# Routing a mixture in quarters of the tokens: more of the next layer beside the expert slots of a two-layer kernel on one core

## The chip, the cores and the metric

The kernel runs on one core of a Trainium2 chip. The metric is the device time of one execution in microseconds (us), taken as the median of several runs; the profile is of one execution, and its span runs from the first to the last instruction of the core. PE is the matrix engine (PEld its weight loads), DVE the vector engine, ACT the scalar engine, POOL the general engine, SP the engine that only issues transfers here.

## The reference

All data are float32. `x` is 2 x 1024 tokens of 256 features, `ctx` 2 x 77 context rows. Two layers of the same shape follow each other:

```python
x = x + L0_xattn(ctx, layernorm(x), ...)      # 16 heads of 64, keys and values from tokens and context
x = x + L0_ffn(layernorm(x), ...)             # 8 experts 256 -> 1024 -> 256 with relu, the best 2 per token, then a norm
x = x + L1_xattn(layernorm(x), ctx, ctx, ...) # 16 heads of 16, queries from tokens, keys and values from the context
x = x + L1_ffn(layernorm(x), ...)             # 8 experts, the best 2: four gated MLPs (256 -> 128 -> 256, silu),
                                              # two copies of x, one relu(x), one zero; plus a causal depthwise conv of width 4
```

In the reference `L0_ffn` computes all experts for all tokens and weighs them; only the two chosen ones have a weight.

## The kernel before

The 2048 tokens are 16 tiles `t` of 128 tokens (8 per batch), four tiles are a block (`NBLK = 4`). `xr` holds the running sum of all tokens in SBUF. Four stages follow each other.

**Layer 0's attention** is the first 1158 us; the change does not touch its code, only what waits for its buffers. Beside it, tokens of blocks 0 and 1 are already routed: each token is scattered twice, once per chosen expert, into the DRAM table `tab_x`, where each expert has its own rows.

**The slots** compute the layer-0 experts. A slot is 128 rows of one expert: `NSLOT = 39` of them hold every case of how tokens spread over experts. Which expert and which rows a slot has is computed on the chip: `first_table` (blocks 0 and 1 alone) for the first `NA = 9` slots, `table` for the rest, ordered so that after `NB = 23` slots all rows of batch 0 are done. `ask_rows(s)` loads a slot's rows into `xs`, and `ask(s)` its bias `bs` and its two weight matrices `w1` and `w2` (1 MB each), all on SP's queue, three slots ahead; `entry` reads the address from the table. `turn_rows` transposes the rows (`px`, then `xT` on DVE), `up` is the first matmul in two halves (`ph`; relu of half 0 on DVE, of half 1 on ACT, into `hT`), `down` the second (`po`), run one slot later; ACT copies the result `y` and stores it to the DRAM table `tab_y`. Weights rotate through four buffers (`fw`, `fw_x`), and through two from slot 30 on. PSUM has 8 banks: three `ps_t` for short transposes and products, two `ps_h`, one `ps_o`, and two more (`ps_x`) that the slots use as a third `ph` and a second `po` bank.

**Per tile, after its slots**: `gather(t)` fetches the two expert results of each token by indirect DMA on POOL's queue, `weigh` adds them, `measure`, `residual`, `shift` and `normal` are the norms around it, `turned` and `queries` make the transposed queries `qT` of layer 1. `todo` lists, by slot, what runs behind a slot; tile `t` of batch 0 is gathered behind slot `NB + t`. For batch 1 the residual is `residual_aside`, on ACT and POOL.

**Layer 1's attention** goes in steps: step `k` is one tile and half of the heads (`score`, `soften`, and one step later `turn_step`; `attend` for a pair `p` of tiles; then `divide`, `turn_back`, `project` per tile). From slot `S1 = 31` on there are two steps per slot, one between the halves of `up` and one behind `down`; when the slots end, at step `K1 = 16`, the steps run alone: the tail. `pre`, `fill` and `rest` hold, by step, what else runs: `pre` before the scores, `fill` and `rest` after the softmax.

**Layer 1's experts** (`Mix`, one per block): `measure`, `values`, `turns`, `choose` (the routing), then for each of four experts `up` (`pg`, silu on ACT, `hid` on DVE) and `down` (`po`, added to `xr` by DVE with the token's weight); `copies` adds the copy and relu experts for one tile, `convolve` and `convolved` the convolution. `at_step` sets the steps: block 0's at 16 to 23, block 1's at every second step from 24 to 38, blocks 2 and 3 at 42 to 57.

PE, DVE, ACT, POOL and, in the slots and after, SP issue in the order written here (`manual_schedule`). An instruction that waits holds those behind it on its engine.

Of the kernel before, what the change touches and what calls it, by code (L numbers as in the profile page):

```python
# [38 lines left out]
NB = 2 * S // TB + E0 - 1  # L39
NK = CAP // TB  # L40
# [9 lines left out]
def tile_two_layers(ctx: ExitStack, tc: tile.TileContext, a: dict, out: bass.AP):  # L50
# [938 lines left out]
    def apart_from(ins, mine, other):  # L989

        tc.declare_no_dep(ins.ins, group=other, reason="rows of other tokens")
        tc.add_to_no_dep_group(mine, ins.ins)

    def gather(t):

        got[t] = []
        for k in range(2):
            y = en.tile([P, D], F32, tag="yt", name="yt", bufs=6)
            ins = nc.gpsimd.indirect_dma_start(  # L999
                out=y,  # L1000
                out_offset=None,
                in_=tab_y[:, :],
                in_offset=bass.IndirectOffsetOnAxis(ap=pos[:, t, k : k + 1], axis=0),
            )
            if t < NT // B:
                apart_from(ins, "gathers", "late_stores")
            got[t].append(y)
# [22 lines left out]

    def residual_aside(t):

        nb, rstd = stat.pop((0, t))
        nc.scalar.activation(acc(t), acc(t), AF.Identity, bias=nb[:, :1], scale=rstd[:, :1])
        nc.gpsimd.tensor_tensor(acc(t), acc(t), gamma, ALU.mult)
        nc.gpsimd.tensor_tensor(xr[:, t, :], xr[:, t, :], acc(t), ALU.add)
# [50 lines left out]
    S1 = 31  # L1087
    K1 = 2 * (NSLOT - S1)
    K2 = K1 + 10
# [5 lines left out]
    slots, extra, first, spare = ExitStack(), ExitStack(), ExitStack(), ExitStack()  # L1095
    fw = slots.enter_context(tc.tile_pool(name="fw", bufs=2, reuse_waits="tile"))
    xp = slots.enter_context(tc.tile_pool(name="b_x", bufs=3, reuse_waits="tile"))
    hp = slots.enter_context(tc.tile_pool(name="b_h", bufs=2, reuse_waits="tile"))
    yp = slots.enter_context(tc.tile_pool(name="b_y", bufs=2, reuse_waits="tile"))

    fw_x = extra.enter_context(tc.tile_pool(name="fw_x", bufs=2, reuse_waits="tile"))
    xe = first.enter_context(tc.tile_pool(name="b_xe", bufs=1, side="right", reuse_waits="tile"))
    ps_x = spare.enter_context(tc.tile_pool(name="b_ps_x", bufs=1, space=PSUM, reuse_waits="tile"))
    at_p = ps_s = mp = None
    later = {}

    def table():

        some, took = plan1["some"], plan1["took"]
        every = blocks(xp, "c", counts(NBLK), 0, NK, ALU.is_gt)  # L1110

        n = xp.tile([1, 2, E0], F32, tag="n", name="n", bufs=1)
        nc.vector.tensor_tensor(n[:, 0, :], some, took, ALU.subtract)
        nc.vector.tensor_tensor(n[:, 1, :], every, some, ALU.subtract)
        cum = xp.tile([1, 2, E0], F32, tag="cum", name="cum", bufs=1)
        nc.vector.tensor_copy(cum, n)
        for e in range(1, E0):
            nc.vector.tensor_tensor(cum[:, :, e : e + 1], cum[:, :, e - 1 : e], n[:, :, e : e + 1], ALU.add)
        nc.vector.tensor_tensor(cum[:, 1, :], cum[:, 1, :], cum[:, 0, E0 - 1 :].to_broadcast([1, E0]), ALU.add)
        yield  # L1120

        d = xp.tile([1, 2, E0], F32, tag="d", name="d", bufs=1)
        nc.vector.tensor_tensor(d, n, cum, ALU.subtract)
        nc.vector.tensor_tensor(d[:, 0, :], d[:, 0, :], took, ALU.add)
        nc.vector.tensor_tensor(d[:, 1, :], d[:, 1, :], some, ALU.add)
        d = d.rearrange("o k e -> o (k e)")
        step = xp.tile([1, 2 * E0], F32, tag="step", name="step", bufs=1)
        nc.vector.tensor_copy(step, d)
        nc.vector.tensor_tensor(step[:, : 2 * E0 - 1], d[:, 1:], d[:, : 2 * E0 - 1], ALU.subtract)
        cum = cum.rearrange("o k e -> o (k e)")  # L1130
        le = xp.tile([1, NL, 2 * E0], F32, tag="le", name="le", bufs=1)
        nc.vector.tensor_tensor(
            le,
            cum.unsqueeze(1).to_broadcast([1, NL, 2 * E0]),
            slot[:1].unsqueeze(2).to_broadcast([1, NL, 2 * E0]),
# [5 lines left out]
        nc.vector.tensor_tensor(le, le, step.unsqueeze(1).to_broadcast([1, NL, 2 * E0]), ALU.mult)  # L1141
# [6 lines left out]
        nc.vector.tensor_tensor(used, slot[:1], cum[:, 2 * E0 - 1 :].to_broadcast([1, NL]), ALU.is_lt)  # L1148
        nc.vector.tensor_tensor(off, off, used, ALU.mult)
        nc.vector.tensor_scalar_mul(off, off, float(TB))  # L1150
        nc.vector.tensor_scalar(used, ex[:, 0, :], float(E0), -float(E0), ALU.is_ge, ALU.mult)
        nc.vector.tensor_tensor(ex[:, 0, :], ex[:, 0, :], used, ALU.add)
# [13 lines left out]
    def ask_rows(s):  # L1166

        r0 = entry(nc.sync, s, 1)
        if s < NA:
            xs = xe.tile([P, D], F32, tag=f"xs{s}", name="xs", bufs=1)  # L1170
        else:
            xs = xp.tile([P, D], F32, tag="xs", name="xs")
        nc.sync.dma_start(out=xs, in_=tab_x[bass.ds(r0, TB), :])
        rows_of[s] = xs

    def ask(s):

        e = entry(nc.sync, s, 0)
        bs = xp.tile([P, NF], F32, tag="bs", name="bs", bufs=4)
        nc.sync.dma_start(out=bs, in_=a["L0_ffn_b1"][:, bass.ds(e * NF, NF)])  # L1180
        pool = fw_x if s % 4 > 1 and s < S1 - 1 else fw
        w1 = pool.tile([P, 2, F0], F32, tag="w1", name="w1")
        nc.sync.dma_start(
            out=w1,
            in_=a["L0_ffn_W1"][bass.ds(e, 1)].rearrange("o k f -> (o k) f").rearrange("(c p) f -> p c f", p=P),
        )
        w2 = pool.tile([P, NF, D], F32, tag="w2", name="w2")
        nc.sync.dma_start(
            out=w2,
            in_=a["L0_ffn_W2"][bass.ds(e, 1)].rearrange("o f d -> (o f) d").rearrange("(c p) d -> p c d", p=P),  # L1190
        )
        parts[s] = bs, w1, w2

    def turn_rows(s):
# [4 lines left out]
        xT = xp.tile([P, 2, TB], F32, tag="xT", name="xT")  # L1199
# [3 lines left out]
    def hidden(s):  # L1203
        return hp.tile([P, NF, TB], F32, tag="hT", name="hT")

    def up(s, xT, hT, half):
        bs, w1, w2 = parts[s]
        f4 = half * 4
        pool = ps_x if (2 * s + half) % 3 == 2 and s < S1 else ps_h
        ps = pool.tile([P, 512], F32, tag="h", name="ph")  # L1210
# [18 lines left out]
    def down(s, hT):  # L1229
        w2 = parts.pop(s)[2]  # L1230
        ps = (ps_x if s % 2 and s < S1 else ps_o).tile([P, 512], F32, tag="o", name="po")
# [6 lines left out]
        if s >= NB:  # L1238
            apart_from(ins, "late_stores", "gathers")
# [44 lines left out]
    def soften(t, c, sc):  # L1284
        pr = pr_of[t, c] = at_p.tile([P, 8, C], F32, tag="pr", name="pr", bufs=3)
# [28 lines left out]
    def attend(p, c):  # L1314
# [12 lines left out]
        raw = raw_of[p, c] = at_p.tile([P, 2, 2 * P], F32, tag="raw", name="raw", bufs=4)  # L1327
# [18 lines left out]
    def turn_back(t):  # L1346
# [4 lines left out]
        aT = aT_of[t] = at_p.tile([P, 2 * P], F32, tag="aT", name="aT", bufs=2)  # L1351
# [14 lines left out]
    class Mix:  # L1366
# [69 lines left out]
        def copies(self, i):  # L1436

            t, h, cw = self.tiles[i], self.h[:, i, :], self.cw
            y = mp.tile([P, D], F32, tag="y", name="y")
            nc.gpsimd.tensor_scalar_mul(y, h, cw[:, i, EM : EM + 1])  # L1440
            nc.gpsimd.tensor_tensor(xr[:, t, :], xr[:, t, :], y, ALU.add)
            nc.gpsimd.tensor_scalar(h, h, 0.0, cw[:, i, EM + 3 : EM + 4], ALU.max, ALU.mult)
            nc.gpsimd.tensor_tensor(xr[:, t, :], xr[:, t, :], h, ALU.add)

        def convolve(self, c):

            if c == 0:
                self.cv = mp.tile([P, 2, 512], F32, tag="cv", name="cv", bufs=2)
# [18 lines left out]
        def up(self, e):  # L1467
            ps = []
            for w in (wg1, wu1):
                ups[0] += 1  # L1470
                pool = ps_x if ps_x is not None and ups[0] % 3 == 0 else ps_h
                ps.append(pool.tile([P, 512], F32, tag="h", name="pg"))
                for c in range(2):
                    nc.tensor.matmul(  # L1474
                        ps[-1],
# [5 lines left out]
            sl = mp.tile([P, 512], F32, tag="sl", name="sl", bufs=2)  # L1481
            nc.scalar.activation(sl, ps[0], AF.Silu)
            hid = self.hid[e] = mp.tile([P, 512], F32, tag="hid", name="hid", bufs=2)
            nc.vector.tensor_tensor(hid, sl, ps[1], ALU.mult)

        def down(self, e):
            hid = self.hid.pop(e)
            po = [
                ps_o.tile([P, 512], F32, tag="o", name="po"),
                ps_t.tile([P, 512], F32, tag="t", name="po")  # L1490
                if ps_x is None
                else ps_x.tile([P, 512], F32, tag="o", name="po"),
            ]
# [20 lines left out]
    ups = [0]  # L1514
# [4 lines left out]

    todo = {  # L1520
        0: [r3.values, r3.turns],
        1: [r3.choose],
        2: [r3.place] + [lambda r=r, i=i: r.scatter(i) for r in (r2, r3) for i in range(4)],
        5: [r2.weigh],
        6: [r3.weigh],
        7: [r2.bias_turn],
        8: [r2.bias_add, r3.bias_turn],
        9: [r3.bias_add],
# [7 lines left out]
    for k in (3, 4, 4):  # L1536
        behind(k, next, steps)
    behind(10, constants, 0)
    behind(11, lambda: spread.setdefault("s", side_spread()))
    behind(14, constants, 1)  # L1540
    behind(20, constants, 2)
    behind(S1 + 1, constants, 3)
    for blk in range(NBLK):
        behind(13 + 2 * blk, shifts, blk)
    for t in range(NT // B):
        n = NB + t
        behind(n, gather, t)
        behind(n + 2, weigh, t)
        behind(n + 2, measure, 0, t)
        behind(n + 3, residual, t)  # L1550
        behind(n + 3, measure, 1, t)
        behind(n + 4, shift, 1, t)
        behind(n + 4, normal, t)
        behind(n + 5, turned, t)
        behind(n + 6, queries, t)


    pre, fill, rest, step_of = {}, {}, {}, {}
# [3 lines left out]

    for p in range(NT // 2):
# [38 lines left out]
    for blk in range(NBLK):  # L1602
        for e in range(EM):
            halves.append((blk, e))
# [148 lines left out]
```

## Time and profile before

| | |
|---|---|
| device time, median of 3 runs (all of them) | 1761.82 us (1760.5, 1761.82, 1764.8) |
| the profiled execution: its time, its span | 1765.13 us, 1763.4 us |
| mean granted clock of PE in it | 0.98 |
| instructions in it | 25084 |
| busy: PE, DVE, ACT, POOL | 1649.9, 1073.9, 715.3, 899.1 us |
| moved by DMA | 151.94 MB |

How to read it: the page gives for each engine the time in which it executed something; a busy PE is not a PE at its peak, since matmuls overlap and the clock can be lower. In its 40 slices (44 us each) a digit is the busy share in tenths, and `PEclk` is the clock granted to PE in tenths. A row of a timeline is: start, duration, engine, line, operation, output<-input, shape, count, and in brackets the idle time before it and what ended that. The line numbers are those of the listing above.

### The profile page before, as it was taken

To read this page: it belongs to the slowest core of one execution; us is meant where nothing else is said; L and a number is where in the kernel's file an instruction comes from. 1 tells how busy PE (TensorE), PEld (TensorE's weight loads), DVE (VectorE), ACT (ScalarE), POOL (GpSimd) and SP (SyncE) were. 2 spreads that over 40 slices of the span, in tenths; PEclk is the share of its full clock that TensorE was granted. 3 is DMA by queue.
4 is the path that set the end of the run, shared out by engine and by line. 5 is a ranking of instruction groups with operands and counts; after the bars stand their busy time and mean duration, and the time that the engine had idled before them with its cause. 6 is when DMAs were issued, how large, how long until landed. Compare 5 with 4: busy or idle time off the path is not lost.

```text
span 1763.4 us, 25084 instructions
## 1 busy us (share of the span) xinstructions
PE 1649.9 (94%) x9346; PEld 1052.9 (60%) x9346; DVE 1073.9 (61%) x2133; ACT 715.3 (41%) x1393; POOL 899.1 (51%) x586
## 2 busy tenths in 40 slices
PE   6999999999999999999999999889999989967887
PEld 3544555555555555565555555568898877744554
DVE  5766766666666667677767766644221554476466
ACT  1544444445444444434444445401121244426541
POOL 1277557757756765776757757212300410176124
PEclk9999999999999999999999999999999999989898
DMA  3011211211211210000000000069889956210000
GB/s 115 24 56 61 80 60 68 72 66 66 84 66 66 72 49 7 13 6 7 18 7 1 17 9 1 1 201 364 290 302 322 321 170 198 91 30 25 1 13 24
DMA packets 124862, 151.94 MB, mean 86 GB/s; under 512 B 13211, under 2 KB 112709, under 8 KB 124741
## 3 DMA queue, kind: packets, MB, share of 16 engines
q1 hardware_dynamic: 79984, 102.18, 17.2%
q10 hardware_dynamic: 41685, 39.77, 6.5%
q0 software_dynamic: 3072, 8.39, 1.4%
q8 instruction: 74, 1.21, 0.3%
q14 instruction: 47, 0.39, 0.1%
HBM read 105.10 MB, written 45.22 MB: 85 GB/s over the span
## 4 chain that ended last, share of the span: by engine, by line
PE 71%; DVE 12%; ACT 7%; POOL 6%; DMA 2%; issue 2%; SPq 0%; ACTq 0%; DVEq 0%
PE sc L745 13%; PE ptr L797 12%; PE po L822 8%; PE po L1233 7%; PE ph L1214 7%; PE pqk L675 7%; DVE nm L755 5%; POOL pa L779 4%; ACT pa L756 4%; PE pv L651 3%; PE py L690 3%; PE pg L1474 3%; PE ptr L1308 1%; PE sb L720 1%; ACT pT L117 1%
## 5 line engine op out<-in xcount | busy, mean ns | idle before, releaser
L779 POOL TENSOR_SCALAR pa<-pa,f 128x1024 f32<-128x1024 f32 x244 | 695.8, 2869 | 363.9 <-ACT pT L117 259.7
L756 ACT ACTIVATE pa<-sc,nm 128x1024 f32<-128x1024 f32 x256 | 283.1, 1110 | 424.6 <-DVE nm L755 424.6
L755 DVE TENSOR_REDUCE nm<-sc 128x1 f32<-128x1024 f32 x256 | 301.4, 1219 | 137.0 <-PE sc L745 137.0
L797 PE MATMUL ptr<-ident,pa 128*128 128x128 f32 x2048 | 286.2, 279 | 25.5 <-DVE kT L121 4.5
L797 PEld LDWEIGHTS ptr<-ident,pa 128*128 128x128 f32 x2048 | 225.9, 141 | 108.8 <-issue 62.9
L822 PE MATMUL po<-pT,v 128*64 128x512 f32 (+1 forms) x1152 | 262.6, 598 | 0.0
L745 PE MATMUL sc<-kT,qT 64*128 64x512 f32 x1024 | 257.3, 621 | 0.0
L121 DVE COPY pT<-ptr 128x512 f32<-128x512 f32 x256 | 175.8, 689 | 100.5 <-PE ptr L797 97.3
L117 ACT COPY pT<-ptr 128x512 f32<-128x512 f32 (+1 forms) x320 | 177.8, 587 | 137.4 <-PE ptr L797 134.0
L822 PEld LDWEIGHTS po<-pT,v 128*64 128x64 f32 (+1 forms) x1152 | 78.3, 136 | 153.9 <-issue 148.9
L1214 PE MATMUL ph<-xT,w 128*128 128x128 f32 x1248 | 151.1, 279 | 7.7 <-DMA w<-in_L_ffn_W_dram 5.6
L1214 PEld LDWEIGHTS ph<-xT,w 128*128 128x128 f32 x1248 | 147.0, 194 | 13.4 <-issue 12.3
L1233 PE MATMUL po<-w,hT 128*128 128x256 f32 x624 | 143.4, 383 | 1.4 <-issue 0.9
L745 PEld LDWEIGHTS sc<-kT,qT 64*128 64x128 f32 x1024 | 89.4, 188 | 84.3 <-issue 80.8
L1233 PEld LDWEIGHTS po<-w,hT 128*128 128x128 f32 x624 | 116.7, 192 | 16.7 <-issue 1.3
L1227 DVE TENSOR_SCALAR hT<-ph,bs 128x128 f32<-128x128 f32 x156 | 43.9, 344 | 108.0 <-PE ph L1214 93.2
L155 POOL TENSOR_TENSOR rstd<-ve,neghalf 128x1 f32<-128x1 f32 (+2 forms) x45 | 32.2, 719 | 146.1 <-DVE ve L148 123.8
L1225 ACT ACTIVATE hT<-ph,bs 128x128 f32<-128x128 f32 x156 | 44.6, 369 | 136.9 <-PE ph L1214 101.2
L999 POOL DMA_INDIRECT yt<-tab_y,pos x32 | 32.1, 1002 | 117.4 <-DMA tab_y<-y 110.0
L651 PE MATMUL pv<-wv,kvT 128*128 128x256 f32 (+1 forms) x288 | 70.9, 389 | 2.9 <-DVE pB L731 2.3
L675 PE MATMUL pqk<-kvT,wk 128*128 128x512 f32 (+1 forms) x192 | 73.1, 510 | 0.0
L651 PEld LDWEIGHTS pv<-wv,kvT 128*128 128x128 f32 (+1 forms) x288 | 53.4, 189 | 25.6 <-issue 16.4
(254 smaller groups left out, 1866.1 us busy)
## 6 DMA issues: line engine op xcount, KB each, us to landing
w<-in_L_ffn_W_dram SPq DMA_DIRECT2D x78, 1024.0 KB
tab_x<-zero ACTq DMA_DIRECT2D x32, 512.0 KB
tab_y<-zero ACTq DMA_DIRECT2D x32, 512.0 KB
xs<-tab_x SPq DMA_DIRECT2D x39, 128.0 KB
tab_y<-y ACTq DMA_DIRECT2D x39, 128.0 KB
xr<-in_x_dram SPq DMA_DIRECT2D x4, 512.0 KB
wq<-in_L_xattn_Wq_dram SPq DMA_DIRECT2D x8, 256.0 KB
wk<-in_L_xattn_Wkv_dram SPq DMA_DIRECT2D x8, 256.0 KB
```

Source lines behind the costliest of these rows:

```text
L117: nc.scalar.copy(dst, src)
L121: nc.vector.tensor_copy(dst, src)
L651: nc.tensor.matmul(ps[:r, n * GC : (n + 1) * GC], kvT[b][:, c, kt * P : kt * P + r], groups[G]["v"][:, c, :], start=(c == 0), stop=(c == 1),)
L675: nc.tensor.matmul(ps[:, : n1 - n0], groups[G][nm][:, c, p * P : (p + 1) * P], kvT[b][:, c, n0:n1], start=(c == 0), stop=(c == 1),)
L745: nc.tensor.matmul(sc[j][:, n * 512 : (n + 1) * 512], U.qT[j * DH0 : (j + 1) * DH0, q0 : q0 + P], U.kT[j * DH0 : (j + 1) * DH0, n * 512 : ...
L755: nc.vector.tensor_reduce(U.nm[:, 0, r : r + 1], sc[j], AX.X, ALU.max, negate=True)
L756: nc.scalar.activation(U.pa[t][:, j, :], sc[j], AF.Exp, bias=U.nm[:, 0, r : r + 1], accum_out=U.l[:, 0, r : r + 1])
L779: nc.gpsimd.tensor_scalar_mul(pa, pa, f)
L797: nc.tensor.transpose(ps[:, n * P : (n + 1) * P], U.pa[t][:, j, kt * P : (kt + 1) * P], ident)
L822: nc.tensor.matmul(U.po[j * DH0 : (j + 1) * DH0, :], v[:r, kt, h0 : h0 + DH0], U.pT[j][:r, kt, :], start=(kt == 0), stop=(kt == NKT - 1),)
L1214: nc.tensor.matmul(ps[:, n * TB : (n + 1) * TB], w1[:, c, f * P : (f + 1) * P], xT[:, c, :], start=(c == 0), stop=(c == 1),)
L1233: nc.tensor.matmul(ps[:, :D], hT[:, f, :], w2[:, f, :], start=(f == 0), stop=(f == NF - 1))
```

## The change

The layer-0 results of three quarters of the tokens, not of half, are now known to be complete before the slots end: `table` orders the slots after the ninth in three groups (rest of batch 0, block 2, block 3), and `NB2 = 31` slots cover tiles 0 to 11. Tiles 0 to 7 are gathered in pairs behind slots 23 to 26, tiles 8 to 11 in pairs behind slots 31 and 32, the last four in the tail; the pieces of a tile's chain (`way`) now lie half a slot apart, since `todo` is read in the middle of a slot too. Steps begin at `S1 = 28`, so `K1` is 22; the last two pairs of tiles follow at steps 29 to 36 (before, the last four pairs at 26 to 41). Block 0's experts run at steps 17 to 24, so the first of them beside slots, block 1's at 25 to 32, block 2's between 33 and 44, block 3's from 46 to 53, where the kernel ends (before: 57).

`ask` can load `w1` and `w2` apart. From slot 28 on `w1` of slot `s + 2` is asked for in slot `s`, and `w2` of slot `s + 1`. The four weight buffers are four pools in a new order, the `xs` tiles of the first slots are allocated in a new order, and for the first two slots `w2` is placed before `w1`; the pools of the slots lie on the other side of SBUF. PSUM is divided once: `ps_s` (two banks) stays through slots and tail, serves odd slots as a second pair of `ph` banks, then the scores, then odd experts of block 3; there is one `po` bank. `copies` does its two scalings on ACT instead of POOL, `residual_aside` is gone (all tiles use `residual`, on DVE). `attend` runs one step later, before `turn_step`. Some buffers are fewer (`pr` 3 to 2, `raw` 4 to 3, `aT` 2 to 1, `cv` 2 to 1, `sl` 2 to 1, shared with `tT`); `hid` uses the places of two old weight tiles; `yt` has 8 instead of 6.

```diff
+NB2 = 3 * S // TB + E0 - 1
...
             if t < NT // B:
-                apart_from(ins, "gathers", "late_stores")
+                apart_from(ins, "gathers", ("later_stores", "last_stores"))
+            elif t < 12:
+                apart_from(ins, "later_gathers", ("last_stores",))
...
-    def residual_aside(t):
-
-        nb, rstd = stat.pop((0, t))
-        nc.scalar.activation(acc(t), acc(t), AF.Identity, bias=nb[:, :1], scale=rstd[:, :1])
-        nc.gpsimd.tensor_tensor(acc(t), acc(t), gamma, ALU.mult)
-        nc.gpsimd.tensor_tensor(xr[:, t, :], xr[:, t, :], acc(t), ALU.add)
...
-    S1 = 31
+    S1 = 28
     K1 = 2 * (NSLOT - S1)
-    K2 = K1 + 10
+    K2 = K1 + 7
...
+    fw = [
+        (ctx if i < 2 else extra).enter_context(tc.tile_pool(name=f"fw{i}", bufs=1, reuse_waits="tile"))
+        for i in range(4)
+    ]
+    xs_of = {s: xe.tile([P, D], F32, tag=f"xs{s}", name="xs") for s in (*range(3, NA), 2, 0, 1)}
...
+        most = blocks(xp, "d", counts(3), 0, NK, ALU.is_gt)
         every = blocks(xp, "c", counts(NBLK), 0, NK, ALU.is_gt)
...
+    def ask(s, *which):
+
+        pool = fw[(2, 1, 0, 3)[s % 4]] if s < S1 else fw[(1, 0)[s % 2]]
         e = entry(nc.sync, s, 0)
...
+        p = parts.setdefault(s, {})
+        if s < 2:
+            p["w2"] = pool.tile([P, NF, D], F32, tag="w2", name="w2")
+        for nm in which or ("w1", "w2"):
+            if nm == "w1":
+                p["bs"] = xp.tile([P, NF], F32, tag="bs", name="bs", bufs=4)
...
+    def ask_later(s):
+
+        if s + 3 < NSLOT and s + 3 >= NA:
+            ask_rows(s + 3)
+        if s + 3 < S1:
+            ask(s + 3)
+        elif s + 3 < S1 + 2:
+
+            ask(s + 3, "w1")
+        if S1 <= s + 2 < S1 + 2:
+            ask(s + 2, "w2")
+        if s >= S1 and s + 2 < NSLOT:
+            ask(s + 2, "w1")
+        if s > S1 and s + 1 < NSLOT:
+            ask(s + 1, "w2")
...
     def hidden(s):
-        return hp.tile([P, NF, TB], F32, tag="hT", name="hT")
+        hT = hp.tile([P, NF, TB], F32, tag="hT", name="hT")
+        if s % 2 and s < S1:
+            ph = ps_s.tile([P, 2, 512], F32, tag="s", name="ph")
+            return hT, [ph[:, 0, :], ph[:, 1, :]]
+        return hT, [ps_h.tile([P, 512], F32, tag="h", name="ph") for _ in range(2)]
...
-            y = mp.tile([P, D], F32, tag="y", name="y")
-            nc.gpsimd.tensor_scalar_mul(y, h, cw[:, i, EM : EM + 1])
+            y = at_p.tile([P, D], F32, tag="y", name="y", bufs=2)
+            nc.scalar.activation(y, h, AF.Copy, scale=cw[:, i, EM : EM + 1])
             nc.gpsimd.tensor_tensor(xr[:, t, :], xr[:, t, :], y, ALU.add)
-            nc.gpsimd.tensor_scalar(h, h, 0.0, cw[:, i, EM + 3 : EM + 4], ALU.max, ALU.mult)
+
+            nc.scalar.activation(h, h, AF.Relu, scale=cw[:, i, EM + 3 : EM + 4])
             nc.gpsimd.tensor_tensor(xr[:, t, :], xr[:, t, :], h, ALU.add)
...
+    def way(t, put):
+
+        put(1, weigh, t)
+        put(1, measure, 0, t)
+        put(2, residual, t)
+        put(2, measure, 1, t)
+        put(3, shift, 1, t)
+        put(3, normal, t)
+        put(4, turned, t)
+        put(5, queries, t)
...
+    def begins(p):
+        return 4 * p if p < 6 else K2 + 4 * (p - 6)
...
-            put(fill, k0 + 2 * c + 2, attend, p, c)
+            put(mid, k0 + 2 * c + 3, attend, p, c)
...
-    K3 = K2 + 16
...
+    K3 = begins(NT // 2 - 1) + 13
+    at_step = [17 + n for n in range(16)] + [33, 34, 35, 37, 38, 40, 42, 44] + [K3 + n for n in range(8)]
```

## The prediction

> **What bounds the kernel now.** I read the page first, then cut the span into stages with the busy-time windows, then walked PE's and SP's timelines.
>
> ```profile
> PE 1649.9 (94%) x9346; PEld 1052.9 (60%) x9346; DVE 1073.9 (61%) x2133; ACT 715.3 (41%) x1393; POOL 899.1 (51%) x586
> PE   6999999999999999999999999889999989967887
> PEclk9999999999999999999999999999999999989898
> DMA  3011211211211210000000000069889956210000
> ```
>
> PE carries the kernel. It is full in every slice but the first and the last five, and there the granted clock drops too. The windows cut that end (columns: stretch, its length, busy time with instruction count on PE, PEld, DVE, ACT, POOL, then clock, DMA share, GB/s).
>
> ```profile
> 1166.00:1385.40 219.40, 214.00 (x1426) 196.77 (x1427) 69.49 (x249) 43.12 (x142) 43.86 (x69) 0.98 0.94 323
> 1385.40:1411.70 26.30, 24.42 (x174) 22.96 (x173) 16.16 (x53) 7.78 (x23) 11.17 (x15) 1.00 0.79 273
> 1411.70:1534.30 122.60, 115.77 (x851) 94.00 (x850) 58.13 (x145) 55.93 (x131) 10.61 (x17) 1.00 0.49 162
> 1534.30:1590.90 56.60, 40.64 (x165) 25.37 (x163) 36.97 (x115) 18.44 (x33) 41.09 (x49) 0.85 0.10 31
> 1590.90:1671.50 80.60, 64.67 (x366) 40.35 (x364) 47.20 (x101) 44.92 (x83) 32.90 (x41) 0.87 0.04 14
> 1671.50:1732.30 60.80, 49.40 (x282) 32.74 (x282) 41.63 (x122) 25.83 (x45) 19.24 (x23) 0.99 0.03 9
> 1732.30:1763.40 31.10, 26.16 (x81) 15.12 (x80) 18.33 (x36) 5.07 (x7) 13.50 (x14) 0.88 0.10 34
> ```
>
> The rows are slots 0 to 27; slots 28 to 30; slots 31 to 38 with attention steps 0 to 15 between their halves; then the tail: steps 16 to 25, 26 to 37, 38 to 49, and block 3's experts (50 to 57). Beside slots PE is over 94% busy at clock 1.00. In the tail's 229.1 us no engine is full: PE is busy for 180.9, DVE for 144.1, and in the first row POOL for 41.09 of 56.60. It is a chain of latencies, and PE pays twice, once idle and once at a low clock:
>
> ```profile
> 1560.25 2.80 PE L1398 MATMUL pt<-ident,h 128*128 128x128 f32 x8 [4.42 <-ACT h L1384]
> 1562.84 3.62 PE L1474 MATMUL pg<-hT,wg 128*128 128x512 f32 x4
> 1582.88 1.12 PE L1464 MATMUL pc<-ident,cv 128*128 128x128 f32 x4 [9.46 <-DVE xr L1503]
> ```
>
> The four pg matmuls take 1.88 elsewhere. Two more losses stand at the slots. Their first loads are asked for only when layer 0's attention has ended (PE's last matmul there ends at 1158.56), and slot 30's w2 request holds SP's queue from 1392.08 to 1400.31, with a row request behind it:
>
> ```profile
> 1158.72 0.37 SPq L1173 DMA_DIRECT2D xs<-tab_x  x1
> 1160.89 0.39 SPq L1183 DMA_DIRECT2D w<-in_L_ffn_W_dram  x1
> 1166.05 6.06 PE L1214 MATMUL ph<-xT,w 128*128 128x128 f32 x32 [4.83 <-DMA w<-in_L_ffn_W_dram]
> 1392.08 0.38 SPq L1183 DMA_DIRECT2D w<-in_L_ffn_W_dram  x1
> 1400.31 0.38 SPq L1188 DMA_DIRECT2D w<-in_L_ffn_W_dram  x1
> 1406.85 0.41 PE L1198 MATMUL px<-ident,xs 128*128 128x128 f32 x2 [1.88 <-DMA xs<-tab_x]
> ```
>
> **The change, part by part.** The work is nearly the same; it moves. Steps begin at slot 28, not 31, so 22 steps instead of 16 lie beside slots, the whole ends at step 53, not 57, and 32 steps, not 42, stay in the tail. PE prices, from start to start in its timeline: a slot 7.25 (two halves of 1.79, px 0.22, down 3.46); per step sc 0.72 and ptr 0.93; o 1.05 every second step; per tile pn 0.53, pt 0.22, py 0.86, and 1.12 for its queries; an expert 3.44 up and 1.72 down; a block's routing 2.6.
>
> *Start of the slots.* Row and weight tiles get other SBUF places. The first xs request waited for oT; that the new places come free earlier, no row shows. At best it wins the two idles (2.25 before px, 4.83 before ph) and the slow first half-slots (6.06 against 3.73): 9.4. At worst nothing, and no loss, since every layer-0 buffer is free by 1158.6. DMA share is 0.00 in 1100:1140, so an early request would land: I take -7.
>
> *Slots 0 to 27.* Same weights and rows. One po bank instead of two: ACT copies y in 0.37 and has 3.8 us until the next down, and ACT was idle 51.9 us before 19 of those copies; nothing. If ACT came late, each microsecond would be one of PE's. Constants move 1.5 slots earlier on SP's queue; the stall around them (PE late by about 2 us near 1350) moves along. New is that tiles 0 to 7 come two per slot. A tile's chain costs DVE four scalar_tensor_tensor of 0.535, two bn_stats of 0.42, two aggregates of 0.18, two of 0.15 and one of 0.25: 3.9. Two tiles and the slot's own 1.55 (hT 1.13, xT 0.42) make 9.3 us in a slot of 7.25, for two slots: +4 (0 to +6).
>
> *Slots 28 to 38.* PE: 11 slots 79.8, one more down 3.5, 22 sc 15.8, 21 ptr 19.5, 10 o 10.5, 8 tiles 12.9, 10 query tiles 11.2, one routing 2.6, and the moved experts (three up, one down) 12.0: 167.8. The same count for slots 31 to 38 before gives 112.5 of the 122.6 measured, so 10 us go to stalls; I keep 10. Weights now wait on two buffers, w1 asked for after the up that frees it (about 14 us ahead; 1 MB at 321 GB/s is 3.3) and w2 after the down (about 28 ahead). Behind a waiting request on SP stand only the next rows, needed over two slots later, so the 4 us lost to xs at slots 30 and 31 go. DVE was 25.56 busy in the 40 us from 1420 (one tile's chain per slot) and 14.47 in the 40 us from 1460 (mostly none), so 9.2 and 5.2 per slot of 14.4; with two tiles 13.2, for about four slots. I add 5 for that: 183 (168 to 200).
>
> ACT alternates Silu and Exp in steps 17 to 23. Each table load took 1283 ns in the 13 rows of the tail; about 7 more are 9 us on an engine 46% busy (55.93 of 122.60). I take nothing (up to 9). The Trainium skill ("ScalarE: Activation LUTs", What ACT_TABLE_LOAD costs) speaks against such interleaving: load and drain together 2.66 us; by it the term would be, as an estimate from that page, 18.6 instead of 9. The trace shows no drain: the load at 1538.19 is followed by its Silu at 1539.49.
>
> *Tail, steps 22 to 32.* At full clock PE has 59 us here: five up and six down 27.5, six sc and six ptr 9.9, o 3, four tiles 6.4, two routings 5.2, four query tiles 4.5, pc 2.4. DVE has about 61. Four tiles are gathered instead of eight, so POOL issues 4 fewer pairs of 1.0 each; it still waits at step 22 for the last store to land (1535.26 to 1537.74 before), with the ln powers queued behind, as before. `copies` takes from POOL 16 times 0.94 and 1.26 (35 us) and gives ACT 32 of at most 0.60 (19 us). Eight `residual_aside` go: 12.6 us of POOL, and DVE gets 8.6. So the 5.04 of DVE waiting for POOL before L1503, and the 9.46 of PE behind it, have no cause left; next late is DVE. Before, this kind of stage kept PE 72 to 80% and DVE 59 to 65% busy. With POOL relieved I take 80 us (59, the content, to 92, DVE's at 65%).
>
> *Steps 33 to 45.* Pair 7's scores to block 3's routing took 60.8. Block 2's experts now start with them instead of four steps later, `attend` runs a step later, so its wait for ACT pT goes; PE has about 41. I take 55 (45 to 61). *Block 3.* Odd experts use the two freed ps_s banks; PE bound at 5.17 an expert: 30 (27 to 31.1).
>
> The clock follows the gaps: 0.85 and 0.87 in the two gappy rows. PE's 105 us there at a full clock would be 15 shorter; the 80 keeps part of that loss. The Trainium skill ("TensorE: Matmul & The Clock Gate", Part 1) has half clock until about 3.4 us of sustained work; by it, an estimate, every long gap costs a further 1.7; the pg row above agrees with 3.62 for 1.88.
>
> **Sum**, in the profiled execution: the start 1166.0 - 7, slots 0 to 27 219.4 + 4, makes 1382.4; + 183 + 80 + 55 + 30 = 1730.4. Its span was 1763.4, so -33.0. It took 1765.1 (1.7 around the span), and the median of the runs is 1761.8, 3.3 below it: 1761.8 - 33.0 = 1728.8; I say 1728.
>
> **Rivals.** (a) *The tail keeps its pace.* DVE's 112 us at the 63% it had (144.1 of 229.1) are 178 instead of 165, and slots 28 to 38 cost their 190s: 1743 to 1757. For it: every stage of the tail was latency-bound. Against: POOL, which held the worst stalls, is relieved.
> (b) *PE stays full.* Stages near their PE content, 172 + 66 + 50 + 28: 1688 to 1710. For it: the 94% beside slots. Against: DVE nearly equals PE in steps 22 to 32.
> (c) *Slower: DVE's queue paces slots 28 to 38.* In-order waits behind two tile chains hold xT and the softmax, and PE with them. The gain of 33 is gone at 3.0 us more for each of 11 slots (over 19.6 instead of 16.6); at 5 more the time is 1784. For it: 13.2 of 14.4 on DVE. Against: that holds for four slots only, and chains are now cut into half-slots.
> (d) *Nothing gained:* the moved PE work is paid in full and the tail's length is set by the last gather's chain: within 0.3% (5 us, about what a measurement of this kernel tells from no change).
>
> **How the numbers follow.** The forecast (1710 to 1742) 0.55, (a) 0.17, (b) 0.13, (c) 0.10, (d) 0.05. Faster is forecast, (a) and (b): 0.85; same 0.05; slower 0.10. The range takes in the forecast, (a) and the upper part of (b), about 0.8: 1700 to 1757.
>
> **What would show it.** Right: ph's first row without the 4.83 before it; SP's w1 and w2 requests never 8 us apart before rows; slots 28 to 38 in about 183 us at clock 1.00; the last down of a slot near 1565; a tail of some 165 us with POOL well under half busy. Wrong: a longer slot beside steps with xT or pr late on DVE, the 4.83 still there, or steps 22 to 32 above 90 us.

## The result and the profile after

The changed kernel takes 1754.2 us (median of 6 runs, 1752.5 to 1757.0) beside 1763.3 for the kernel before (6 runs on the same chips): ratio 0.9948, 95% interval 0.9932 to 0.9965. It is faster, by 9 us where 33 were forecast. The time lies inside the stated range, but not in the forecast case. It falls among the times of rival (a), though not for its reasons: slots 28 to 38 did not cost its 190s, and the tail, which did about keep its pace, came out 5 us above the forecast. The profiled execution's span is 1751.6 us against 1763.4.

The page first: busy time and slices of PE, its granted clock and the DMA engines, then PE's group line for the up matmuls (count, busy, mean ns; then the idle time just before them and what ended most of it), and last the same group line of the kernel before.

```profile
PE 1636.5 (93%) x9348; PEld 1050.5 (60%) x9348; DVE 1079.8 (62%) x2149; ACT 735.9 (42%) x1425; POOL 850.0 (49%) x538
PE   6998999999999999999999999898999899997887
PEclk9999999999999999999999999999999999998989
DMA  3011211211211210000000010087798737420000
...
L1244 PE MATMUL ph<-xT,w 128*128 128x128 f32 x1248 | 155.4, 281 | 27.7 <-DVE hT L1257 24.1
...
L1214 PE MATMUL ph<-xT,w 128*128 128x128 f32 x1248 | 151.1, 279 | 7.7 <-DMA w<-in_L_ffn_W_dram 5.6
```

POOL is down by 49 us in the whole. The group line holds the surprise: PE idled 27.7 us ahead of its up matmuls, and 24.1 of that ended on `hT`, a product of the very matmuls it holds up. Before, the same group had idled 7.7 us, 5.6 of them ended by weight loads. The windows by stage, cut where the prediction cut them (columns as there: stretch, length, busy on PE, PEld, DVE, ACT, POOL, clock, DMA share, GB/s):

```profile
1157.00:1378.10 221.10, 200.01 (x1329) 183.13 (x1330) 64.50 (x235) 40.07 (x132) 40.81 (x65) 0.98 0.83 282
1378.10:1404.80 26.70, 20.09 (x121) 18.25 (x120) 20.08 (x64) 5.63 (x17) 16.22 (x21) 0.87 0.63 220
1404.80:1581.50 176.70, 171.28 (x1219) 138.54 (x1218) 100.11 (x259) 90.90 (x202) 31.28 (x44) 0.99 0.44 143
1581.50:1668.60 87.10, 64.27 (x353) 42.37 (x351) 60.05 (x168) 46.35 (x83) 24.00 (x33) 0.91 0.07 21
1668.60:1722.30 53.70, 47.06 (x241) 30.05 (x240) 28.79 (x62) 29.53 (x47) 6.79 (x9) 0.92 0.03 11
1722.30:1751.60 29.30, 23.86 (x82) 14.35 (x81) 21.21 (x56) 9.01 (x16) 6.15 (x8) 1.00 0.11 36
```

The rows are slots 0 to 25; slots 26 and 27; slots 28 to 38; steps 22 to 32; steps 33 to 45; block 3. The last three are the tail: it is shorter (170.1 us for 229.1) but hardly denser, with PE busy for 79% of it as before and DVE for 65% (63% before). Beside the prediction, and beside the first experiment (run A below), in us of the profiled execution:

| stage | predicted | after | run A |
|---|---|---|---|
| first ph of slot 0 starts at | 1159.0 | 1157.0 | 1157.9 |
| slots 0 to 27 (before: 219.4) | 223.4 | 247.8 | 219.1 |
| slots 28 to 38 | 183 | 176.7 | 178.1 |
| steps 22 to 32 | 80 | 87.1 | 86.9 |
| steps 33 to 45 | 55 | 53.7 | 53.4 |
| block 3 | 30 | 29.3 | 29.4 |
| span | 1730.4 | 1751.6 | 1724.8 |

From predicted to after the rows differ by -2.0, +24.4, -6.3, +7.1, -1.3 and -0.7, together +21.2. The missing gain is one row, and it lies where the change seemed to do nearly nothing. PE's timeline there, an even slot and then an odd one (start, duration, instruction and count, idle time before and its releaser):

```profile
1313.95 3.73 PE L1244 MATMUL ph<-xT,w 128*128 128x128 f32 x32
1317.52 0.38 PE L1225 MATMUL px<-ident,xs 128*128 128x128 f32 x2
1317.74 3.62 PE L1263 MATMUL po<-w,hT 128*128 128x256 f32 x16
1321.19 1.95 PE L1244 MATMUL ph<-xT,w 128*128 128x128 f32 x16
1324.42 2.05 PE L1244 MATMUL ph<-xT,w 128*128 128x128 f32 x16 [1.28 <-DVE hT L1257]
...
1388.18 2.05 PE L1244 MATMUL ph<-xT,w 128*128 128x128 f32 x16 [2.69 <-DVE xT L122]
...
1394.77 3.79 PE L1244 MATMUL ph<-xT,w 128*128 128x128 f32 x16 [3.91 <-DVE hT L1257]
```

The even slot runs its 32 up matmuls in one go. The odd slot runs 16 and stops for 1.28 us until DVE has read half 0 (its four `hT`, 1.13 us together), and only then begins half 1. The last two rows are slot 27, where `hT` stood behind the two tiles' gather chains on DVE and the stop grew to 3.91; slots 5 and 7, with stops of 3.51 and 2.53, are the other long ones (in slot 5 DVE was still computing `table`). The waits of PE in that stretch sum up (total us, times, longest):

```profile
PE ph L1244 <- DVE hT L1257: 24.1, 14, 3.9
```

Fourteen waits, one for each odd slot. In those slots `hidden` puts both halves into one two-bank tile of `ps_s`; in even slots it takes two one-bank tiles of `ps_h`. Half 1 writes another bank than the one DVE reads, and yet it waits.

### The profile page after: what moved, and what is told of

Its sections match the earlier page's. It is cut to its first block, busy times and chain, and to the rows that moved or that the text cites. A ratio compares the mean times of both kernels' runs of the same rounds, so it can differ in the third digit from the quotient of the medians.

```text
span 1751.6 us, 25136 instructions
## 1 busy us (share of the span) xinstructions
PE 1636.5 (93%) x9348; PEld 1050.5 (60%) x9348; DVE 1079.8 (62%) x2149; ACT 735.9 (42%) x1425; POOL 850.0 (49%) x538
## 4 chain that ended last, share of the span: by engine, by line
PE 70%; DVE 13%; ACT 8%; POOL 5%; issue 2%; DMA 1%; ACTq 0%; DVEq 0%; POOLq 0%
PE sc L746 13%; PE ptr L798 12%; PE po L823 8%; PE ph L1244 7%; PE po L1263 7%; PE pqk L676 7%; POOL pa L780 5%; DVE nm L756 5%; ACT pa L757 4%; PE pv L652 3%; PE py L691 3%; PE pg L1508 2%; PE ptr L1340 1%; PE sb L721 1%; ACT pT L118 1%
## 5 line engine op out<-in xcount | busy, mean ns | idle before, releaser
L1244 PE MATMUL ph<-xT,w 128*128 128x128 f32 x1248 | 155.4, 281 | 27.7 <-DVE hT L1257 24.1
L1473 POOL TENSOR_TENSOR xr<-xr,y 128x256 f32<-128x256 f32 x16 | 11.9, 746 | 133.2 <-ACT y L1472 128.1
```

The costliest lines, as they stand in the source:

```text
L1244: nc.tensor.matmul(ps[:, n * TB : (n + 1) * TB], w1[:, c, f * P : (f + 1) * P], xT[:, c, :], start=(c == 0), stop=(c == 1),)
```

## The experiments

**Theory 1:** the shared tile is the loss. The wait follows from the program: half 1's matmuls write a tile that DVE, earlier in program order, reads; whole tiles are ordered, not banks. **Rival 2:** the loss comes with the place, the `ps_s` banks or a single `po` bank, and would stay if only the tile were split. **Rival 3:** DVE's doubled gather chains or the weight traffic slow these slots, and the wait is only where it shows. Comparisons go by the ratio to the kernel before, run beside each.

**A. The halves in two tiles, in the same banks.** A spare pool of two one-bank tiles is open until slot 28; `ps_s` opens in its place after that. That the banks are the same follows from the order in which the pools are opened; the trace does not show bank numbers.

```diff
         if s % 2 and s < S1:
-            ph = ps_s.tile([P, 2, 512], F32, tag="s", name="ph")
-            return hT, [ph[:, 0, :], ph[:, 1, :]]
+            return hT, [ps_x.tile([P, 512], F32, tag="h", name="ph") for _ in range(2)]
```

> The changed kernel, but an odd slot's two halves of ph take two tiles of one bank each (the same two banks until slot 28, given back before the scores take them), not one tile of two banks. Theory 1 (the wait is one of the shared tile: half 1's matmuls are held until DVE has read half 0, because both halves are one tile): the 14 waits of PE for hT, 24.1 us in all, go; slots 0 to 25 take 205 to 208 us instead of 221.1, the whole falls by 16 to 26 us, to 1728 to 1738. Theory 2 (a limit of the memory: PE writing one bank while DVE reads its neighbour): nothing changes, since banks and accesses are the same, 1754. Theory 3 (the slots are slower because loads or DVE come late): nothing changes.

Measured: 1728.9 us, ratio 0.9817 (0.9796 to 0.9837). PE's timeline, odd and even slot alike:

```profile
1244.04 3.73 PE L1244 MATMUL ph<-xT,w 128*128 128x128 f32 x32
1247.61 0.38 PE L1226 MATMUL px<-ident,xs 128*128 128x128 f32 x2
1247.83 3.62 PE L1263 MATMUL po<-w,hT 128*128 128x256 f32 x16
1251.28 3.73 PE L1244 MATMUL ph<-xT,w 128*128 128x128 f32 x32
```

Odd and even slots alike now take 7.24, as before the change; the `hT` waits are gone, and slots 0 to 27 take 219.1. The windows (slots 0 to 25, slots 26 and 27):

```profile
1157.88:1354.99 197.11, 194.33 (x1329) 179.63 (x1329) 64.04 (x234) 39.98 (x132) 40.01 (x65) 1.00 0.90 304
1354.99:1376.95 21.96, 18.81 (x122) 17.47 (x120) 16.76 (x52) 5.65 (x17) 15.85 (x20) 0.92 1.05 366
```

The place, the banks and the gather chains are those of the changed kernel. Rivals 2 and 3 fall for all but slots 26 and 27, which still cost 22.0 where they cost 14.5 before. Slots 0 to 25 take 197.1 where they took 204.9 before. Of these 7.8 us the earlier loads explain 2.2, in slot 0 (6.47 from its first up to the next slot's, for 8.69). Another 5.4 lie in slots 3 and 4 (15.02 for 20.45), where PE stood in short stops (put down to `issue`) in the profiled execution before. C below starts its loads as late as that kernel and has no such stops; what caused them stays open.

**B. All slots in `ps_h`.** The plain undoing of this part.

```diff
-        if s % 2 and s < S1:
-            ph = ps_s.tile([P, 2, 512], F32, tag="s", name="ph")
-            return hT, [ph[:, 0, :], ph[:, 1, :]]
         return hT, [ps_h.tile([P, 512], F32, tag="h", name="ph") for _ in range(2)]
```

> The changed kernel, but all slots, odd ones too, take ph from the two ps_h banks, each half its own tile; the two other banks are unused until slot 28. Theory 1: the same fall as with the split tile, 16 to 26 us, to 1728 to 1738, since a slot of 7.25 us leaves DVE and ACT time to empty two banks. If more banks were needed (the reason for a second pair): 1740 or more, with PE waiting for hT at the start of a half. Theory 2: a fall too, as the banks are no longer neighbours in use at once in odd slots alone. Theory 3: 1754.

Measured: 1728.1, ratio 0.9805 (0.9787 to 0.9824), and again in another set 1731.6, 0.9828 (0.9805 to 0.9851). Two banks do as well as four: these slots need no more banks, but halves that don't share a tile. The second set, which ended just above its expected ratio, was run beside D's repeat:

> The kernel with all slots on ps_h and tiles in pairs, again: ratio 0.978 to 0.982 to the kernel before, as in its first three rounds.

**C. The shared tile alone, in the kernel before.** Odd slots get `after`'s two-bank tile, and the downs one `po` bank.

```diff
+        if s % 2 and s < S1:
+            ph = ps_x.tile([P, 2, 512], F32, tag="s", name="ph")
+            return hT, [ph[:, 0, :], ph[:, 1, :]]
+        return hT, [ps_h.tile([P, 512], F32, tag="h", name="ph") for _ in range(2)]
...
+        ps = ps_o.tile([P, 512], F32, tag="o", name="po")
```

> The kernel before, with this one part of the change alone: an odd slot's two halves of ph are one tile of two banks, even slots take ps_h, and there is one po bank. Theory 1: odd slots (15 before slot 31) wait some 1.3 us each for DVE and lose about 1.5: +20 to +26 us, 1783 to 1789. Theory 2: the same. Theory 3: 1763, no change.

Measured: 1781.0, ratio 1.0115 (1.0093 to 1.0137), so some 20 us slower, about the lower end of what was expected. The waits of PE over the slots, and two of them:

```profile
PE ph L1217 <- DVE hT L1230: 20.4, 15, 2.5
```
```profile
1228.88 2.05 PE L1217 MATMUL ph<-xT,w 128*128 128x128 f32 x16 [2.53 <-DVE hT L1230]
...
1247.36 2.05 PE L1217 MATMUL ph<-xT,w 128*128 128x128 f32 x16 [1.28 <-DVE hT L1230]
```

The same steady 1.28 in a kernel that has nothing else of the change but the single `po` bank, and no wait of PE for that bank shows. Splitting the tile wins some 23 us of the changed kernel (0.9948 to 0.9817 of the time before), and adding it costs the old kernel 20.

**H. The shared tile kept, DVE's reads later in program order.** This asks whether the wait lies in the chip (an engine reading beside another's writes) or in the order of the program. In odd slots the four relus of half 0 are written after half 1's matmuls.

```diff
+        late = s % 2 == 1 and s < S1
...
+        for n in range(4):
+            if half and late:
+                src = pss[0][:, n * TB : (n + 1) * TB]
+                nc.vector.tensor_scalar(hT[:, n, :], src, bs[:, n : n + 1], 0.0, ALU.add, ALU.max)
...
-            else:
+            elif not late:
                 nc.vector.tensor_scalar(hT[:, f, :], src, bs[:, f : f + 1], 0.0, ALU.add, ALU.max)
```

> The changed kernel with its shared two-bank tile, but in odd slots DVE's four relu of half 0 are written in the program behind half 1's matmuls, not ahead of them. Theory 1a (a write to a tile is held for the reads of that tile that stand ahead of it in the program, whatever part they read): half 1 waits for nothing, slots 0 to 25 again in 205 to 210 us, 1728 to 1738 in all; DVE starts its relu 1.8 us later, which nothing on PE waits for. Theory 1b (the tile is held while anyone still uses it, also in time): PE waits as in the changed kernel, 1754.

Measured: 1735.4, ratio 0.9828 (0.9811 to 0.9845). The same tile, banks and reads, and PE's row has no stop:

```profile
1251.03 3.73 PE L1246 MATMUL ph<-xT,w 128*128 128x128 f32 x32
...
1258.28 3.73 PE L1246 MATMUL ph<-xT,w 128*128 128x128 f32 x32
```

So the stop goes with the program order on one tile. Whether the chip would have let both engines at the two banks at once H can't say, since its reads come later; A can. There, PE's first row above (slot 11, an odd one: 1244.04 to 1247.77, its half 1 from about 1245.8, by the 1.79 us of a half) runs on through DVE's reads of half 0:

```profile
1246.08 1.13 DVE L1257 TENSOR_SCALAR hT<-ph,bs 128x128 f32<-128x128 f32 x4 [4.87 <-PE ph L1244]
```

The memory allows it; the order that the program fixes for the shared tile doesn't.

**D. Tiles 0 to 7 gathered one per slot**, on top of B, for the slower slots 26 and 27.

```diff
-        h0 = 2 * (NB if t < 8 else NB2) + 1 + (t if t < 8 else t - 8) // 2 * 2
-        late = 3 if t < 8 else 1
+        h0 = 2 * (NB + t) + 1 if t < 8 else 2 * NB2 + 1 + (t - 8) // 2 * 2
+        late = 2 if t < 8 else 1
```

> As the kernel in which all slots take ps_h, and besides tiles 0 to 7 are gathered one per slot (behind slots 23 to 30, the chain a half-slot tighter), not in pairs behind 23 to 26. If two tiles' chains in slots of 7.25 us hold DVE back (slots 26 and 27 took 26.7 us against 14.5 before): these two slots fall to 16 to 19, the whole by a further 5 to 10 us against the kernel with pairs. If the delay of slots 26 and 27 came from the shared tile as well, pairs and single tiles are within 3 us.

> The kernel with all slots on ps_h and one tile per slot, again, beside the one with pairs on the same chip: if two tiles' chains per slot cost what slots 26 to 29 showed, its ratio is 0.002 to 0.004 below that of the pairs.

Measured: 1725.5, ratio 0.9794 (0.9774 to 0.9814), and again 1727.3, 0.9799 (0.9773 to 0.9824). Against B the medians fall by 2.7 and 4.3 us; the intervals overlap, so this stays likely rather than settled. The stage was not the expected one: slots 0 to 27 take 219 in both, since slot 26 in D stands 3.64 us behind `xT`. What fell is slots 28 to 38 (window from 0.4 us behind the start of slot 28, then steps 22 to 32):

```profile
1380.00:1554.97 174.97, 170.04 (x1223) 137.38 (x1222) 106.89 (x281) 90.37 (x202) 39.24 (x54) 1.00 0.47 154
1554.97:1641.70 86.73, 65.61 (x353) 43.48 (x351) 60.03 (x168) 46.32 (x83) 23.98 (x33) 0.91 0.07 21
```

Here they take 175 where B took 181 and A 178, in one profiled execution each. By its medians D is the fastest version run, and clearly faster than both kernels; its lead over A (1728.9, intervals overlapping) is not settled either.

**E. The old order of the first loads**, on B: row tiles, weight pools and the order of w1 and w2 requests as before, on the new side of SBUF.

```diff
-    xs_of = {s: xe.tile([P, D], F32, tag=f"xs{s}", name="xs") for s in (*range(3, NA), 2, 0, 1)}
+    xs_of = {s: xe.tile([P, D], F32, tag=f"xs{s}", name="xs") for s in range(NA)}
...
-        pool = fw[(2, 1, 0, 3)[s % 4]] if s < S1 else fw[(1, 0)[s % 2]]
+        pool = fw[s % 4] if s < S1 else fw[(1, 0)[s % 2]]
-        if s < 2:
-            p["w2"] = pool.tile([P, NF, D], F32, tag="w2", name="w2")
...
-                if s > 1:
-                    p["w2"] = pool.tile([P, NF, D], F32, tag="w2", name="w2")
+                p["w2"] = pool.tile([P, NF, D], F32, tag="w2", name="w2")
```

> As the kernel in which all slots take ps_h (1728), but rows and weights of the first slots are placed in the old order: xs tiles 0 to 8 in their order, the four weight pools in theirs, w1 ahead of w2 in every slot. If the new places are why the first loads no longer wait for the end of layer 0's attention: the gap before the first up returns in part or in whole, +3 to +8 us, 1731 to 1736. If the order does not matter (the pools' new side alone does it): 1728.

Measured: 1733.8, ratio 0.9823 (0.9805 to 0.9841), within the noise of B. SP's and PE's rows at the start:

```profile
1113.70 0.37 SPq L1178 DMA_DIRECT2D xs<-tab_x  x1
1133.31 0.38 SPq L1191 DMA_DIRECT2D w<-in_L_ffn_W_dram  x1
```
```profile
1154.75 0.38 PE L1222 MATMUL px<-ident,xs 128*128 128x128 f32 x2
1156.03 3.84 PE L1238 MATMUL ph<-xT,w 128*128 128x128 f32 x32 [0.90 <-DVE xT L122]
```

Of the two cases expected, the second came: the chip of this set was slower (1767.1 for the kernel before), and by the ratio there is no loss beyond the noise. The requests go out 45 and 28 us earlier than before the change without the new order of tiles. With that order they go out earlier still (the first `xs` request at 1027.63), and nothing is gained by it. What E keeps is enough: the new side of SBUF and the four weight pools in place of two. These two were not tried apart.

**F. The scalings of `copies` back on POOL**, on B.

```diff
-            nc.scalar.activation(y, h, AF.Copy, scale=cw[:, i, EM : EM + 1])
+            nc.gpsimd.tensor_scalar_mul(y, h, cw[:, i, EM : EM + 1])
...
-            nc.scalar.activation(h, h, AF.Relu, scale=cw[:, i, EM + 3 : EM + 4])
+            nc.gpsimd.tensor_scalar(h, h, 0.0, cw[:, i, EM + 3 : EM + 4], ALU.max, ALU.mult)
```

> As the kernel in which all slots take ps_h (1728), but copies does its two scalings on POOL again. If POOL's relief is what shortens steps 22 to 32: +4 to +10 us, 1732 to 1738, POOL over 35 us busy in those steps instead of 24. If POOL is no longer on the path now that only four tiles are gathered there: within 3 us of 1728.

Measured: 1740.9, ratio 0.9857 (0.9836 to 0.9878) against B's 0.9805 and, in its second set, 0.9828: this part of the change is worth 5 to 9 us. Against E, which ran beside it and does as well as B, it is 7.1. The intervals of F and of B's second set overlap a little. Steps 22 to 32 of F, then of B:

```profile
1563.90:1654.40 90.50, 70.04 (x355) 45.01 (x353) 61.79 (x168) 42.23 (x73) 38.13 (x46) 0.86 0.06 20
```
```profile
1559.24:1646.40 87.16, 64.36 (x353) 42.39 (x351) 60.03 (x168) 46.31 (x83) 24.02 (x33) 0.91 0.07 20
```

POOL carries 14 us more in this window, and the window takes 3.3 more; the steps behind it add 1.3. The rest is not placed: F's slots 0 to 27 are 4.9 longer than B's too, but so are E's, by 4.6, with `copies` unchanged.

**G and K. What holds steps 22 to 32 at 87.** Both were built on D. After the change PE stops there before the transposes `pc`, behind DVE's `xr`:

```profile
1611.32 1.12 PE L1497 MATMUL pc<-ident,cv 128*128 128x128 f32 x4 [8.26 <-DVE xr L1534]
...
1667.59 1.11 PE L1497 MATMUL pc<-ident,cv 128*128 128x128 f32 x4 [6.03 <-DVE xr L1534]
```

G lets the convolution of blocks 0 to 2 come two steps later (first diff). K takes the taps from the second on from DVE in these blocks: ACT scales and POOL adds (second diff; to make room, the gathers' `yt` has 6 buffers, not 8).

```diff
-                put(rest, k[1], m.convolved, i)
+                put(rest, k[1] + 2 * (blk < NBLK - 1), m.convolved, i)
```
```diff
             for k in range(1, KC):
+                if self.blk < 3:
+                    tap = at_p.tile([P, 512], F32, tag="tap", name="tap")
+                    nc.scalar.activation(
+                        tap, src[:, k : k + 512], AF.Copy, scale=cw1[:, c * KC + k : c * KC + k + 1]
+                    )
+                    nc.gpsimd.tensor_tensor(cv, cv, tap, ALU.add)
+                    continue
```

> As the kernel with one tile per slot (1725), but the four pc turns of blocks 0 to 2 (convolved) run two steps later, so that PE does not stand at the fourth pc while DVE is behind with the routing and the last tiles' chains. If those two stops (6.6 and 6.0 us) are PE's own loss: -5 to -10 us, 1715 to 1720. If DVE is the bound there and the stop only moves to another instruction: within 3 us of 1725.

> As the kernel with one tile per slot, but the three later taps of the convolution of blocks 0 to 2 leave DVE (three scalar_tensor_tensor of 0.85 us per call, 15 us in all): ACT scales a tap into a buffer, POOL adds it; six yt buffers instead of eight, for the space. If DVE is what bounds steps 22 to 32 (60 of 87 us busy there, PE standing at pc behind it): the stage falls by 4 to 9 us and the whole to a ratio 0.003 to 0.006 below that kernel's. If it is the order of the chains (the wait for ACT, POOL or PE inside them) and DVE is only where it shows: within 0.002, or slower by the longer way over ACT and POOL.

Measured: G 1742.9, ratio 0.9858 (0.9837 to 0.9879); K 1740.8, ratio 0.9880 (0.9859 to 0.9901). D had 0.9794 and, beside K, 0.9799: both lose over 10 us. G ran beside E (1733.8), and is 9 slower than that as well. Its stops changed place:

```profile
1592.31 1.93 PE L1349 MATMUL o<-pT,v1p 77*32 77x256 f32 x16 [5.38 <-DVE xr L1531]
...
1606.16 0.69 PE L1494 MATMUL pc<-ident,cv 128*128 128x128 f32 x2 [3.81 <-DVE xr L1495]
```

K's window, then two of its stops on PE, and what ACT did ahead of the first of them:

```profile
1555.00:1653.70 98.70, 68.02 (x353) 44.48 (x350) 53.81 (x160) 53.89 (x95) 36.84 (x44) 0.87 0.06 18
```
```profile
1568.40 2.08 PE L1427 MATMUL pt<-ident,h 128*128 128x128 f32 x8 [6.08 <-ACT aT L1381]
...
1634.69 1.11 PE L1427 MATMUL pt<-ident,h 128*128 128x128 f32 x4 [5.31 <-ACT pT L1338]
```
```profile
1565.27 0.72 ACT L1487 ACTIVATE tap<-hT,cw 128x512 f32<-128x512 f32 x1 [1.82 <-POOL cv L1490]
1567.37 0.72 ACT L1487 ACTIVATE tap<-hT,cw 128x512 f32<-128x512 f32 x1 [1.37 <-POOL cv L1490]
1567.99 0.35 ACT L1381 COPY aT<-pt 128x256 f32<-128x256 f32 x1
```

DVE fell from 60.0 to 53.8 us and the stage grew from 86.7 to 98.7, and the new stops come from ACT, which also evicts `aT` and `pT`: it waited for POOL's adds with those evictions queued behind. PE's two stops before `pc` stayed (13.6 us, for 12.6 in D). Of the two cases expected for K the second came, slower by the longer way over ACT and POOL, and by more than I thought. K does not show what a less busy DVE alone would do, since it also lengthens the chain (and has fewer `yt` buffers); whether DVE's load or the order of the chains sets the 87 us stays open.

## Why the prediction was right and wrong

**Start of the slots, -7: right in size.** From the end of PE's last layer-0 matmul to the first ph it was 7.5 us and is 1.1, where the term left 0.5; PE no longer waits for weights and rows. The further 2.7 us by which the slots start earlier in the profiled execution are layer 0's own end, which the change was not meant to move. Which edit does it was left open there; E narrows it to the pools' side and number.

**Slots 0 to 27, +4 (0 to +6): this step failed.** It measured +28.4. The step began "Same weights and rows" and went through what was added in DVE, ACT and SP: the gather chains, the single `po` bank, the constants. The diff line that puts `ph` of odd slots into a two-bank tile was never priced. It looked like a change of address: the matmuls, their operands and the banks' independence stay. What it changes is who must have finished before half 1 may start, and that costs the length of DVE's four reads plus their latency, 1.28 us, once in every odd slot, and more when DVE is late. A takes the row back to 219.1; C and H show the cause from the other side. Nothing could hide it, as PE itself was the engine held.

**The rest of that step: in part luck.** A's 219.1 lies at the lower bound of the term, but not for its reasons. Slots 26 and 27 took 7.5 us more (22.0 for 14.5), above the term's bound of 6. The wait that it described is there (2.44 us for `xT` behind the chains), but so are 2.6 us of PE's own work for the queries of two tiles: the sum counts ten tiles of queries in slots 28 to 38 and four in the tail, and leaves out these two. Against this stand the 7.8 us of slots 0 to 25, of which the change is shown to have won only the 2.2 in slot 0. D shows that one chain per slot leaves slots 0 to 27 at 219 as well.

**Slots 28 to 38, 183: 176.7.** The 5 us for DVE were not needed: PE is busy for 171.3 of it at clock 0.99, and DVE for 100.1. So rival (c), DVE pacing these slots, did not occur. SP's queue still showed long stops, against the sign I had named: a w2 request goes out at 1403.24, 15.9 us after the row request before it (1387.34). This one belongs to the late slot 27: in A the same request follows its rows by 3.0 us. Others stay in A, the longest 16.3 us, where a w request waits for PE to be done with its buffer. The sign was badly chosen, for none of them cost anything: the rows asked for behind them were not late, and no px waits for a load in this stage.

**Steps 22 to 32, 80: 87.1.** Inside the bounds (59 to 92) and the term's direction is right, F giving the relief of POOL its price. The 80 assumed that DVE would be next late and busy for 61 of 80 us, 76%. It is busy for 60.05 of 87.1, or 69%, close to the 65 and 59% of such rows before: the content was right, the density was not. G and K tried two ways to make it denser and lost; why the stage is no denser stays open. The longest pc stop is still 8.26 us, where I had said that the 9.46 had no cause left.

**Steps 33 to 45 and block 3** came within 1.3 us of 55 and 30.

**Rivals.** (a) named the right number, but the loss lies in a stage that it did not name. Its tail was half right: DVE is busy for 65% of the tail, near the 63% of (a) rather than the 68% in the forecast, and the 170.1 us lie between the 165 of the forecast and the 178 of (a). Its slots 28 to 38 in the 190s did not come. (b) and (d) did not occur. With the tile split, or with B or D, the kernel runs at 1725 to 1729 on the chip where the kernel before took 1761.8: the sum had 1728.8 for it. The rest of the sum stands in total, and that is partly luck: its terms are off by -4.9 to +6.9 and cancel (A's span ends 5.6 below it).

## What to carry to other kernels

Price every new PSUM tile by who reads it before it is written next in program order: in this program a tile over several banks is one object to the ordering, and the engine that fills its second part waits for the readers of its first. Give each half its own tile, or write the readers behind all writers. And before work is taken off a busy engine in a stage of chains, look for what else stands in the receiving engine's queue.

## What the runs showed of the hardware

PE's writes to one PSUM bank and DVE's reads of another go side by side: in A's slot 11 the 1.13 us of reads lie inside PE's unbroken 3.73. The Trainium skill ("PSUM — Partial Sum Buffer", PSUM bank collisions) says that two engines on different banks run clean together, and A agrees.

A long stop can cost twice. In the changed kernel the 16 up matmuls behind the stops of 3.51 and 3.91 us took 3.78 and 3.79 us instead of 1.95, and behind stops of 1.28 to 2.69 us they took 2.05:

```profile
1203.72 3.78 PE L1244 MATMUL ph<-xT,w 128*128 128x128 f32 x16 [3.51 <-DVE hT L1257]
...
1223.66 2.05 PE L1244 MATMUL ph<-xT,w 128*128 128x128 f32 x16 [2.53 <-DVE hT L1257]
```

The granted clock was 0.87 in the window of slots 26 and 27, with the 3.91 in it, and 0.98 in the window of slots 0 to 25. The length of the stop alone does not decide: in A 16 of them took 2.86 behind a stop of 2.44.

Work moved off a busy engine can lengthen its stage: in K DVE was 6.2 us less busy than in D, and the stage 12.0 us longer.
